# All values first in the second projections of a decoder layer, and the late half of a norm spread over two projections

## The chip, the cores and the metric

The kernel runs on one core of one Trainium2 chip. The metric is device time in microseconds (us) of one execution. The core has TensorE (PE, matrix products), VectorE (DVE) and ScalarE (ACT) for elementwise work, GpSimd (POOL), and SyncE (SP), from whose queue nearly all DMAs of this kernel are issued. PSUM banks hold the products of PE until ACT or DVE have read them.

## What is computed

One decoder layer in float32 on x (8 batches of 100 tokens, 1024 features) and a context of 8 x 722 tokens:

```python
x = layernorm(x + retention_attention(x))            # 8 heads, rope, gated, out projection
# cross attention: 16 query heads, 4 key/value heads of 128
q = rms_norm(x @ wq); k = rms_norm(x @ wk); v = x @ wv
k_ctx = rms_norm(ctx @ wk_ctx); v_ctx = ctx @ wv_ctx
q, k = rope(q), rope(k)
probs = softmax(q @ concat(k_ctx, k).T * scale + mask)
x = layernorm(x + (probs @ concat(v_ctx, v)) @ wo)
x = layernorm(x + (silu(x @ w_gate.T) * (x @ w_up.T)) @ w_down.T)
```

## The kernel before

Features lie on the 128 partitions, and the 800 tokens are worked in two halves of N = 400. Every float32 operand of a large product is split into a high part (an ACT cast) and a low part (a DVE subtraction; both are `split2`, line 68), and a product is three matmuls (`mm3`, lines 90, 93 and 94). `proj` multiplies a weight of 1024 x 128 with one half of the normed activations z: 8 steps of 3 matmuls into one PSUM bank. PSUM has three banks of tag "a", four of tag "s" and one of tag "v". `load_w` loads a weight into one of three staging tiles (`wst`) and splits it into one of four `w` tiles.

A scheduler of the framework orders the instructions of each engine ahead of time by its own simulation; on the chip every engine runs its instructions in that order. `pin` (`keep_in_program_order`) keeps the pinned instructions in the order of the program among themselves, and `issue_after(x)` puts what is issued within it behind x.

`out_proj` makes the output projection and the layer norm behind it, and is used twice: after the first attention (its z feeds the second projections) and after the cross attention (its z feeds the first products of the feed-forward part). For each half it computes eight blocks y[m]. The second half's norm is split. `norm_early`, in the middle of the eighth block, takes the mean of the first seven blocks (a product with `onem7`, L345), subtracts it (L347) and squares. What is left goes as a table of steps, `todo`, to the projection after it: the eighth block's share `delta` as a product (L302) before step QT = 4 of `proj`, the variance (L302) before step 7, and with it `late`: `norm_late` (L353, L356, L358), the inverse root (L127 to L135) and `scaled` (L322), which scales the eight blocks, splits them into z and writes them out.

The second projections (tile pool `l2`) are, for each of the four key/value heads kv, weights w2[kv, 0..3] for queries, w2[kv, 4] for keys and w2[kv, 5] for values. They go in groups of weights: for kv = 0 the four queries, then key and value; for the others two, two and two. Within a group come the first half of the tokens for all its weights, then the second. The very first projection, w2[0, 0] on the first half, is the one that carries `todo`. A query or key is squared on ACT (L701), summed over the partitions on POOL (L140), turned by rope (ACT copies L148 and L149; DVE products L150, L151 and sum L152; L150 is the last DVE reader of its bank), scaled by the inverse root (L127 to L135, L706), split into `d` and written out to `qd` or `kd`. A value is copied to `vt` by ACT (L160), transposed by PE in four pieces (L163), split into `vs` and written to `vd`.

The first batch's context is loaded and split by `load_context(0)`, called before the second group: eight loads of a `cs` tile (of the `wst` staging tiles), each with a split into `big`. The context's keys for kv = 0 and 1 are projected between the groups (`context_keys`), with weights read back from `wcd`.

In the feed-forward part the weights w3[i, part] for i = 0, 1 (gate and up) are multiplied with z of the first half and then of the second; the very first of these projections carries the second norm's `todo`.

Of the kernel before, what the change touches and what calls it, by code (L numbers as in the profile page):

```python
# [18 lines left out]
NB = 4  # L19
# [21 lines left out]
def decoder_layer(ctx, tc, xT, cT, w1, wo1, w2, wo2, wc, w3, wd, gw, qw, kw, trig, dec, mask, out):  # L41
# [68 lines left out]
            return True  # L110
        return False

    def proj(w, z, n=N, tag="a", todo=None):
        acc = bank(tag)[:, :n]
        for k in range(KT):
            pinned = between(todo, k)
            t = z[k // QT]
            mmw(acc, w, k, t[:, 0, k % QT, :n], t[:, 1, k % QT, :n], k == 0, k == KT - 1, pinned)
        return acc
# [32 lines left out]
        nc.vector.tensor_tensor(t1, t1, t2, op)  # L152
        return t1

    def tokens_first(pool, acc, copied=True):

        vt = acc
        if copied:
            vt = pool.tile([P, N], F32, tag="vt", name="vt", bufs=1)
            nc.scalar.copy(vt, acc)  # L160
        tr = bank("s")
        for b in range(NB):
            nc.tensor.transpose(tr[0:T, b * P:(b + 1) * P], vt[:, b * T:(b + 1) * T], ident)  # L163
        return tr[0:T]
# [70 lines left out]
    def out_proj(half, w, load_o, res, yp, ybufs, p, make_z, dst, z, steps={}):  # L235


        og = load_o(half)
        y = None
        s1 = p.tile([P, N], F32, tag="s1", name="s1", bufs=2)  # L240
        early = {}
        first = 4 if half == 0 else 1
        for ms in [range(first)] + [[m] for m in range(first, KT)]:
            accs = [bank(("aaasaaaa", "sssaaass")[half][m])[:, :N] for m in ms]
            todo = steps.get(ms[0])
            if half == 1 and KT - 1 in ms:
                todo = {QT: lambda: early.update(norm_early(y, s1, p))}
            for c in range(2):
                for m, acc in zip(ms, accs):
                    wt = load_w(w[m, c])  # L250
                    for k in range(KT):
                        kt = c * KT + k
                        pinned = between(todo, k) if c == 0 and m == ms[0] else False
                        rh, rl = og(kt)
                        a = acc if len(rh.shape) == 2 else bt(acc)
                        mmw(a, wt, k, rh, rl, kt == 0, kt == 2 * KT - 1, pinned)
            if y is None:
                y = yp.tile([P, KT, N], F32, tag="y", name="y", bufs=ybufs)
            for m, acc in zip(ms, accs):
                rs = yp.tile([P, N], F32, tag="rs", name="rs", bufs=2)  # L260
                nc.sync.dma_start(out=rs, in_=res[half, :, m])
                if early:
                    nc.vector.tensor_tensor(rs, rs, early["mean"], ALU.subtract)
                    with tc.high_priority():
                        nc.vector.tensor_tensor(y[:, m], acc, rs, ALU.add)
                else:
                    nc.vector.tensor_tensor(y[:, m], acc, rs, ALU.add)
                    add_up(s1, y, m)


        kept = {}

        def centre():
            kept["mean"] = bank("s")[:, :N]
            pin(nc.tensor.matmul(kept["mean"], onem, s1, start=True, stop=True))

        def less(ms):
            for m in ms:
                nc.vector.tensor_tensor(y[:, m], y[:, m], kept["mean"], ALU.subtract)
            kept["sq"] = squares(y, p, ms, kept.get("sq"))  # L280

        def whole():
            var = bank("v")[:, :N]
            pin(nc.tensor.matmul(var, onem, kept["sq"], start=True, stop=True))
            z.append(make_z(half))
            scaled(y, inv_root(p, var, eps_ln), lambda m: dst[half, :, m], z[half])

        def late():
            norm_late(y, early, p)
            z.append(make_z(half))  # L290
            scaled(y, inv_root(p, early["vs"], eps_ln), lambda m: dst[half, :, m], z[half])

        if half == 0:
            return {0: {QT: centre}, 1: {QT: lambda: less(range(QT))}, 2: {QT: lambda: less(range(QT, KT))},
                    4: {QT: whole}}, y
        sq = squares(y, p, [KT - 1])
        return {QT: lambda: summed(early["delta"], y[:, KT - 1], True, True),
                KT - 1: lambda: (summed(early["var"], early["sq"], True), summed(early["var"], sq, False, True), late())}, y

    def summed(acc, x, start=False, stop=False):  # L300

# [15 lines left out]
                s2 = s3  # L317
        return s2

    def scaled(y, r, dst, z=None):  # L320
        for m in range(KT):
            nc.vector.scalar_tensor_tensor(y[:, m], y[:, m], -0.5, r, ALU.mult, ALU.mult)  # L322
            if z is not None:
                split(z[m // QT][:, :, m % QT], y[:, m])
            nc.sync.dma_start(out=dst(m), in_=y[:, m])

    def norm_root(y, s1, p):
        n = y.shape[2]
# [289 lines left out]

    z1pool = sbuf("z1", 4)
    z1p = z1pool.__enter__()  # L620

    with sbuf("ln1", 1) as p:
        z1, todo = [], {}
        for half in range(2):
            todo, _ = out_proj(half, wo1, load_o1, xT, p, 2, p, lambda _: [
                z1p.tile([P, 2, QT, N], FR, tag="z", name="z") for _ in range(2)], zd, z1, todo)
        ws2 = [load_w(w2[0, 0])]
        acc2 = [proj(ws2[0], z1[0], todo=todo)]


    kapool = sbuf("ka", 2, "right")
    ka = kapool.__enter__()
    cz = []

    def load_context(b):

        cz.clear()
        for hf in range(2):
            n = SN[hf]
            z = [big([P, 2, QT, SH]) for _ in range(2)]  # L640
            for k in range(0, KT, 2):
                cs = wp.tile([P, KT * P], F32, tag="wst", name="cs", bufs=3)
                cs = cs[:, :2 * n].rearrange("p (k n) -> p k n", k=2)
                nc.sync.dma_start(out=cs, in_=cT[b, :, k:k + 2, hf * SH:hf * SH + n])
                split(z[k // QT][:, :, k % QT:k % QT + 2, :n], cs)
            cz.append(z)

    def context_keys(kv):

# [26 lines left out]


    early = []
    with sbuf("l2", 2) as p:
        for kv in range(NKV):  # L680
            for i0, i1 in ((0, 4), (4, 6)) if kv == 0 else ((0, 2), (2, 4), (4, 6)):
                if (kv, i0) == (0, 4):
                    load_context(0)
                ws = [ws2.pop() if ws2 else load_w(w2[kv, i]) for i in range(i0, i1)]
                if (kv, i0) in ((1, 2), (2, 2)):
                    step, kept = context_keys(kv - 1)
                    early.append(kept)
                if (kv, i0) in ((1, 2), (2, 0), (2, 2), (3, 0)):
                    step(i0 == 0)
                for half in range(2):  # L690
                    bs = slice(half * NB, (half + 1) * NB)
                    for i in range(i0, i1):
                        acc = acc2.pop() if acc2 else proj(ws[i - i0], z1[half])
                        if i == 5:
                            tr = tokens_first(p, acc).rearrange("p (b d) -> p b d", b=NB)
                            vs = p.tile([T, NB, 2, P], FR, tag="vs", name="vs", bufs=1)
                            split2(vs[:, :, 0], vs[:, :, 1], tr)
                            nc.sync.dma_start(out=f32(vd[kv, :, bs]), in_=f32(vs))
                            continue
                        sq = p.tile([P, N], F32, tag="sq", name="sq")  # L700
                        nc.scalar.activation(sq, acc, AF.Square)  # L701
                        ss = all_red(p, sq, "ss")
                        tb = tq if i < 4 else tk
                        t = rope(p, acc, tb[:, 0], tb[:, 1], swapped=bank("s")[:, :N])
                        r = inv_root(p, ss, eps_k, at=bank("s")[:, :N])
                        nc.vector.scalar_tensor_tensor(  # L706
                            t, t, -0.5 if i < 4 else -0.5 * math.sqrt(P), r, ALU.mult, ALU.mult)
                        d = p.tile([P, NB, 2, T], FR, tag="d", name="d", bufs=3)
                        split2(d[:, :, 0], d[:, :, 1], bt(t))
                        nc.sync.dma_start(out=f32(qd[kv, i, :, bs] if i < 4 else kd[kv, :, bs]), in_=f32(d))  # L710
    z1pool.__exit__(None, None, None)


# [157 lines left out]
    with sbuf("lnp2", 1) as p:  # L871
        z2, todo = [], {}
        for half in range(2):
            todo, y = out_proj(half, wo2, load_o2, zd, y2p, 1, p, make_z2, zd2, z2, todo)
        w0 = load_w(w3[0, 0])
        acc3 = [proj(w0, z2[0], tag=acc_tag(), todo=todo)]
        mixed2(y)
    zb["b11"], zb["b21"], zb["b22"] = z2[0][0], z2[0][1], z2[1][1]

# [5 lines left out]


    C = ("c11", "c12", "c21", "c22")
    ws = [[w0 if i == part == 0 else load_w(w3[i, part]) for part in range(2)] for i in range(2)]
    gs = {}
    for half in range(2):  # L890
        for i in range(2):
            ag, au = [acc3.pop() if acc3 else proj(w, z2[half], tag=acc_tag()) for w in ws[i]]
            t = temp()
            nc.scalar.activation(t, ag, AF.Silu)
            nc.vector.tensor_tensor(t, t, au, ALU.mult)
# [319 lines left out]
```

## Time and profile before

| | us |
|---|---|
| median of 4 runs | 2502.68 (2501.89 to 2506.67) |
| the profiled execution | 2503.55 |
| its span, first to last instruction | 2501.7 |
| PE busy | 2463.3 (98%) |
| DVE busy | 1950.2 (78%) |
| ACT busy | 1342.4 (54%) |
| POOL busy | 465.6 (19%) |

The profile is of one execution. Busy times are the union of an engine's instructions; a busy PE includes time at a lower granted clock. "Idle before" names the engine whose instruction ended an idle stretch. All positions in time below are microseconds from the start of the span. The first output projection ends at about 583, the second projections at about 837, the second output projection at about 1727.

### The profile page before, as it was taken

How to read it: one execution, taken by the hardware profiler on the slowest of the kernel's cores; microseconds unless marked ns; L12 is line 12 of the kernel's file. 1: busy time of each engine (PE TensorE's matmuls, PEld its weight loads, DVE VectorE, ACT ScalarE, POOL GpSimd, SP SyncE). 2: the span in 40 equal slices, each digit the busy share in tenths (PEclk: the TensorE clock that was granted, in tenths of full speed). 3: DMA queues.
4: the chain of work that ended last, by engine and by line, in shares of the span. 5: the costliest groups of instructions: out<-in, count | busy, mean ns of one | idle time of the engine just before them, and what ended most of it. 6: DMA issues, size and time to landing. Idle time of an engine off the chain costs nothing.

```text
span 2501.7 us, 37219 instructions
## 1 busy us (share of the span) xinstructions
PE 2463.3 (98%) x14068; PEld 2442.7 (98%) x14068; DVE 1950.2 (78%) x3101; ACT 1342.4 (54%) x2258; POOL 465.6 (19%) x234
## 2 busy tenths in 40 slices
PE   9999999997999999999999999999999999999997
PEld 9999999997999999999999999998999999999997
DVE  7778877567877688998999999857977777666756
ACT  6666676335777565665656656534544544432221
POOL 0111111002455343443433433100000000000000
PEclk9999999998999999999999999999999999999999
DMA  7333445774443654454455554565445444388731
GB/s 242 111 111 128 137 144 184 239 269 142 170 148 129 207 191 155 151 177 162 158 168 161 167 175 152 176 239 175 140 171 193 168 166 168 124 287 316 281 103 53
DMA packets 224451, 433.98 MB, mean 173 GB/s; under 512 B 47338, under 2 KB 168042, under 8 KB 211854
## 3 DMA queue, kind: packets, MB, share of 16 engines
q1 hardware_dynamic: 222542, 426.87, 50.2%
q0 software_dynamic: 1152, 4.19, 1.0%
q8 instruction: 111, 1.82, 0.3%
q14 instruction: 70, 0.57, 0.1%
q10 hardware_dynamic: 576, 0.52, 0.1%
HBM read 322.18 MB, written 109.35 MB: 172 GB/s over the span
## 4 chain that ended last, share of the span: by engine, by line
PE 95%; DVE 2%; DMA 1%; ACT 1%; POOL 0%; issue 0%; SPq 0%; DVEq 0%; ACTq 0%
PE a L94 20%; PE a L90 20%; PE a L93 20%; PE s L94 9%; PE s L93 9%; PE s L90 9%; PE v L94 2%; PE v L90 2%; PE v L93 2%; PE s L541 1%; PE s L744 1%; PE s L163 1%; DVE y L322 1%; PE v L533 0%; DMA w<-wcd 0%; POOL ss L140 0%
## 5 line engine op out<-in xcount | busy, mean ns | idle before, releaser
L90 PE MATMUL a<-big,w 128*128 128x400 f32 (+2 forms) x1808 | 609.6, 338 | 2.6 <-DMA w<-wcd 1.2
L93 PE MATMUL a<-big,w 128*128 128x400 f32 (+2 forms) x1808 | 609.2, 337 | 0.2 <-DVE big L68 0.2
L94 PE MATMUL a<-big,w 128*128 128x400 f32 (+2 forms) x1808 | 607.6, 337 | 0.4 <-DVE w L68 0.4
L68 ACT CAST w<-wst 128x1024 fp32r<-128x1024 f32 (+1 forms) x231 | 239.7, 1038 | 387.9 <-PE s L94 148.2
L68 DVE TENSOR_TENSOR w<-wst,w 128x1024 fp32r<-128x1024 f32 (+1 forms) x231 | 282.0, 1221 | 144.4 <-ACT w L68 142.9
L90 PEld LDWEIGHTS a<-big,w 128*128 128x128 f32 x1808 | 339.7, 188 | 5.1 <-DVE s L135 1.8
L93 PEld LDWEIGHTS a<-big,w 128*128 128x128 f32 x1808 | 340.2, 188 | 2.1 <-DVE big L68 0.8
L94 PEld LDWEIGHTS a<-big,w 128*128 128x128 f32 x1808 | 340.2, 188 | 1.2 <-DVE w L68 0.6
L90 PE MATMUL a<-z,w 128*128 128x400 f32 x680 | 236.0, 347 | 15.3 <-DVE t L150 15.3
L94 PE MATMUL a<-z,w 128*128 128x400 f32 x680 | 236.4, 348 | 0.0
L93 PE MATMUL a<-z,w 128*128 128x400 f32 x680 | 236.0, 347 | 0.0
L90 PE MATMUL s<-big,w 128*128 128x400 f32 x664 | 229.9, 347 | 0.1
L94 PE MATMUL s<-big,w 128*128 128x400 f32 x664 | 228.7, 346 | 0.4 <-DVE w L68 0.4
L93 PE MATMUL s<-big,w 128*128 128x400 f32 x664 | 228.9, 345 | 0.0
L140 POOL PARTITION_ALL_REDUCE ss<-sq x56 | 151.5, 2707 | 325.1 <-DMA zd<-y 166.1
L661 POOL PARTITION_ALL_REDUCE kss<-ksq x64 | 167.4, 2616 | 130.7 <-ACT ksq L660 130.1
L90 PEld LDWEIGHTS a<-z,w 128*128 128x128 f32 x680 | 128.8, 189 | 16.7 <-DVE t L150 13.8
L778 ACT ACTIVATE s<-s,rk 128x400 f32<-128x400 f32 x160 | 87.9, 592 | 93.6 <-DVE sm L798 67.2
L94 PEld LDWEIGHTS a<-z,w 128*128 128x128 f32 x680 | 129.4, 190 | 0.2
L93 PEld LDWEIGHTS a<-z,w 128*128 128x128 f32 x680 | 128.7, 189 | 0.5
L90 PEld LDWEIGHTS s<-big,w 128*128 128x128 f32 x664 | 124.6, 188 | 1.6 <-ACT w L68 0.4
L94 PEld LDWEIGHTS s<-big,w 128*128 128x128 f32 x664 | 125.1, 188 | 0.7 <-DVE w L68 0.7
(355 smaller groups left out, 5439.9 us busy)
## 6 DMA issues: line engine op xcount, KB each, us to landing
wst<-in_w SPq DMA_DIRECT2D x135, 512.0 KB
w<-wcd SPq DMA_DIRECT2D x64, 1024.0 KB
wst<-in_wo SPq DMA_DIRECT2D x64, 512.0 KB
hd<-h SPq DMA_DIRECT2D x12, 1400.0 KB
wst<-in_wd SPq DMA_DIRECT2D x64, 256.0 KB
big<-o1d SPq DMA_DIRECT2D x16, 800.0 KB
qd<-d SPq DMA_DIRECT2D x32, 400.0 KB
q<-qd SPq DMA_DIRECT2D x32, 400.0 KB
```

Source lines behind the costliest of these rows:

```text
L68: return nc.scalar.copy(hi, src), nc.vector.tensor_tensor(lo, src, f32(hi), ALU.subtract)
L90: i = nc.tensor.matmul(acc, lh, rh, start=start, stop=False, skip_group_check=chain)
L93: nc.tensor.matmul(acc, lh, rl, start=False, stop=False, skip_group_check=chain)
L94: nc.tensor.matmul(acc, ll, rh, start=False, stop=stop, skip_group_check=chain)
L140: nc.gpsimd.partition_all_reduce(y, x, P, op)
L163: nc.tensor.transpose(tr[0:T, b * P:(b + 1) * P], vt[:, b * T:(b + 1) * T], ident)
L322: nc.vector.scalar_tensor_tensor(y[:, m], y[:, m], -0.5, r, ALU.mult, ALU.mult)
L541: nc.tensor.matmul(bt(o)[:, b], vv[:, b * P:(b + 1) * P], pf[:, b], start=True, stop=True)
L661: nc.gpsimd.partition_all_reduce(ss[:, at], sq[:, at], P, RED.add)
L744: nc.tensor.transpose(tr[0:rows, (c - c0) * P:(c - c0 + 1) * P], vt[:, c * P:c * P + rows], ident)
L778: nc.scalar.activation(sc, sp, AF.Copy, scale=rk[:, c:c + 1])
```

## The change

- In the second projections a first group holds the value weights of all four kv. Their projections on the first half stand within the norm: `todo` is now a table per projection, delta before step 4 of the first, the variance before step 2 of the second, and `late` is called once the second value's products are issued. The first matmul of these two projections is pinned.
- `own_values` does what the loop did for a value, from a pool `v0` of its own, with two `vs` tiles. `late` gets the ACT copy of the second value, and each split of z stands behind it. The values of kv = 2 and 3 stand behind the last ACT cast of z.
- After the values of the second half come, for each kv, two queries, then two queries and the key.
- `load_context(0)` becomes `context_steps`: one of the eight load-and-split steps is issued ahead of each of the projections 4 to 11 (counted from the first value), from two staging tiles in pool `l2`, and each split stands behind the split pair of the projection before.
- In the feed-forward part the first two projections carry the norm's steps in the same way, and `late` follows both, without an instruction to stand behind.

```diff
-    def proj(w, z, n=N, tag="a", todo=None):
+    def proj(w, z, n=N, tag="a", todo=None, pinned=False):
         acc = bank(tag)[:, :n]
+        first = pinned
         for k in range(KT):
-            pinned = between(todo, k)
+            pinned = between(todo, k) or first and k == 0
...
-        return {QT: lambda: summed(early["delta"], y[:, KT - 1], True, True),
-                KT - 1: lambda: (summed(early["var"], early["sq"], True), summed(early["var"], sq, False, True), late())}, y
+        return {0: {QT: lambda: summed(early["delta"], y[:, KT - 1], True, True)},
+                1: {2: lambda: (summed(early["var"], early["sq"], True), summed(early["var"], sq, False, True))},
+                "late": late}, y
...
-            if z is not None:
+            if z is not None and behind is not None:
+                with tc.issue_after(behind.ins):
+                    cast = split(z[m // QT][:, :, m % QT], y[:, m])[0]
+            elif z is not None:
                 split(z[m // QT][:, :, m % QT], y[:, m])
...
+    def own_values(kv, half, acc):
+        got = []
+        tr = tokens_first(v0, acc, True, 1, got).rearrange("p (b d) -> p b d", b=NB)
+        vs = v0.tile([T, NB, 2, P], FR, tag="vs", name="vs")
+        last = split2(vs[:, :, 0], vs[:, :, 1], tr)
+        nc.sync.dma_start(out=f32(vd[kv, :, half * NB:(half + 1) * NB]), in_=f32(vs))
+        return got[0], last
...
-        ws2 = [load_w(w2[0, 0])]
-        acc2 = [proj(ws2[0], z1[0], todo=todo)]
+        ws2 = [load_w(w2[kv, 5]) for kv in range(NKV)]
+        for kv in range(NKV):
+            acc = proj(ws2[kv], z1[0], todo=todo.get(kv), pinned=kv < 2)
+            if kv < 2:
+                got, behind = own_values(kv, 0, acc)
+            else:
+                with tc.issue_after(cast.ins):
+                    got, behind = own_values(kv, 0, acc)
+            if kv == 1:
+                cast = todo["late"](got)
...
+                cs = pool.tile([P, KT * P if behind is None else 2 * SH], F32, tag="wst", name="cs", bufs=bufs)
...
+                    with tc.issue_after(behind[0].ins), tc.issue_after(behind[1].ins):
+                        split(to, cs)
...
-        for kv in range(NKV):
-            for i0, i1 in ((0, 4), (4, 6)) if kv == 0 else ((0, 2), (2, 4), (4, 6)):
-                if (kv, i0) == (0, 4):
-                    load_context(0)
+    groups = [[(kv, 5) for kv in range(NKV)]]
+    for kv in range(NKV):
+        groups += [[(kv, i) for i in range(2)], [(kv, i) for i in range(2, 5)]]
+    unit = NKV
...
+        ctx0 = context_steps(0, p, 2, behind)
+        for g, group in enumerate(groups):
+            ws = ws2 if g == 0 else [load_w(w2[kv, i]) for kv, i in group]
+            if g in (2, 5):
+                step, kept = context_keys(len(early))
+                early.append(kept)
+            if g in (2, 3, 5, 7):
+                step(g in (3, 7))
+            for half in range(g == 0, 2):
+                bs = slice(half * NB, (half + 1) * NB)
+                for (kv, i), w in zip(group, ws):
+                    if 4 <= unit < 12:
+                        next(ctx0)
+                    acc = proj(w, z1[half])
+                    unit += 1
+                    if i == 5:
+                        behind[:] = own_values(kv, half, acc)[1]
+                        continue
...
-        w0 = load_w(w3[0, 0])
-        acc3 = [proj(w0, z2[0], tag=acc_tag(), todo=todo)]
+        w0 = [load_w(w3[0, part]) for part in range(2)]
+        acc3 = [proj(w0[u], z2[0], tag=acc_tag(), todo=todo[u], pinned=True) for u in range(2)]
+        todo["late"]()
```

## The prediction

> **What bounds the kernel now.** I read the page's busy times first, then the list of waits for TensorE (PE), then the stretches around its waits, then the timelines of VectorE (DVE) and ScalarE (ACT) there.
>
> ```profile
> PE 2463.3 (98%) x14068; PEld 2442.7 (98%) x14068; DVE 1950.2 (78%) x3101; ACT 1342.4 (54%) x2258; POOL 465.6 (19%) x234
> ```
>
> PE is the bound: 2501.7 - 2463.3 = 38.4 us idle in all, some of it at the start and the end. No other engine can give anything except through PE's waits, so the next view is the waits (total, times, longest, in us).
>
> ```profile
> PE a L90 <- DVE t L150: 15.3, 2, 13.5
> PE s L93 <- DVE f L68: 3.0, 1, 3.0
> PE s L90 <- ACT f L68: 2.2, 1, 2.2
> PE a L90 <- DMA w<-wcd: 1.2, 2, 0.6
> ```
>
> The 15.3 us are two waits in the second projections, where a projection needs an accumulator bank that rope's first product (L150) still has to read. The 2.2 and 3.0 us lie at the start of the feed-forward part, where PE waits for the normed second half (tile f). These are the two places that the change touches. The same stretches by time show what a wait costs beside itself (columns: PE, PEld, DVE, ACT, POOL busy, then the granted clock, DMA share, GB/s):
>
> ```profile
> 596.00:609.50 13.50, 0.04 (x1) 0.00 (x0) 13.43 (x27) 8.04 (x16) 3.35 (x1) 0.65 0.71 252
> 609.50:613.30 3.80, 3.79 (x11) 3.75 (x12) 1.02 (x2) 1.78 (x4) 3.80 (x2) 0.50 0.00 0
> 638.00:640.00 2.00, 0.12 (x2) 0.07 (x1) 2.00 (x3) 1.01 (x3) 1.11 (x1) 1.00 0.38 148
> 640.00:644.50 4.50, 4.50 (x17) 4.47 (x18) 4.50 (x7) 3.05 (x6) 2.60 (x1) 0.62 0.36 117
> 780.00:828.00 48.00, 48.00 (x265) 48.00 (x264) 37.33 (x69) 34.97 (x70) 26.07 (x11) 1.00 0.47 164
> 1742.20:1748.30 6.10, 0.96 (x4) 0.48 (x3) 6.03 (x13) 4.34 (x9) 0.00 (x0) 0.89 0.57 179
> 1748.30:1753.00 4.70, 4.67 (x14) 4.63 (x15) 4.70 (x10) 3.19 (x6) 0.00 (x0) 0.50 0.94 332
> ```
>
> The row 780 to 828 is the undisturbed pace: 48.0 / 265 = 0.181 us a matmul, so a projection of 24 matmuls (a unit from here on) takes 4.35 us. After each wait the clock stands at 0.50 for some microseconds: lost are 3.8 x 0.50 = 1.9, 4.5 x 0.38 = 1.7 and 4.7 x 0.50 = 2.35 us (with the 0.95 of the next 7 us, 2.7). So the waits and their clock cost 13.47 + 1.9 + 1.88 + 1.7 = 19.0 us at the first place and 2.18 + 2.99 + 2.7 = 7.9 us at the second. 26.9 us is the ceiling of what this change can bring.
>
> Why the long wait exists is in DVE's and PE's timelines:
>
> ```profile
> 601.12 3.97 DVE L322 SCALAR_TENSOR_TENSOR y<-y,r 128x400 f32<-128x400 f32 x8
> 605.01 3.96 DVE L68 TENSOR_TENSOR z<-y,z 128x400 fp32r<-128x400 f32 x8
> 608.90 0.56 DVE L150 TENSOR_TENSOR t<-a,tq 128x400 f32<-128x400 f32 x1
> ...
> 609.51 0.70 PE L90 MATMUL a<-z,w 128*128 128x400 f32 x1 [13.47 <-DVE t L150]
> ```
>
> From 583.3 (the end of the last output projection) PE does three units on the first half's z, fills the three banks of tag a, and stops at 596.0: the rope of the first query stands behind the whole norm on DVE.
>
> **The change part by part.** Same matmuls, transposes, casts and bytes; only places and order move. I take the new order with the durations of before.
>
> *Values first, within the norm (first place).* A value needs no rope: ACT copies the bank (0.49 us, L160), PE turns it (4 transposes in 0.35 us), ACT casts (0.59) and DVE subtracts (0.69). Banks are thus freed by ACT, which was busy 8.0 of the 13.5 us. The 14 z matmuls that stood before the mean (573.55 to 576.1) can't go there any more, as unit 0 is pinned; PE reaches the mean at 573.7. Its operand s1 was ready at 572.8, so no wait, and the mean, with DVE's chain behind it, comes 2.5 us earlier. Last output projection: ends 583.3 - 2.5 = 580.8. Unit 0's first 12 matmuls: 582.9. Delta (0.7): 583.6. 12 + 6 matmuls: 586.9, where the variance stands. Its operand: before, DVE went from the first L347 (576.96) to the last sum of squares (590.5) in 13.6 us, of which 2.5 were three context splits and 1.25 an idle time for one; without these 9.9 us, from 574.5 to 584.4, or 585.6 with one more weight split. So it is there 1.3 us early; I book 0.7 us for a small wait, bounds 0 and 3.6 (a 1.9 us wait with the 1.7 us of clock that the wait at 638 cost).
>
> Variance 1.3 us: 588.2. Then, as before, subtraction, Ln, Exp, Square and two DVE steps: 595.3 to 601.1 = 5.8 us before, of which 1.3 went to a context split in front; so scaling starts at about 592.7 and z's eight parts are done by about 601.4 (8 us, and one value's 0.69). PE meanwhile: 18 matmuls of unit 1 to 591.5, units 2 and 3 to 600.2, transposes 0.7: it asks for the first part of z at 600.9, when seven of eight are there, and takes one each 0.54 us. No wait, with little to spare at the last part. The cover here is the four value units, 17.4 us; were it gone, the 13.5 us would be back.
>
> The added waits: z's casts stand behind the copy of value 1 (at about 592.0, before the first scaled y: nothing). Values 2 and 3 stand behind the last z cast (about 601); behind them on PE wait transposes, and the bank of value 2 is needed by the unit that starts at 605: 3 us to spare. The second vs tile takes away a wait that ACT had for vd's write (2.9 us in 780 to 828), off PE's path: nothing.
>
> *Weights and SP's queue.* Four value weights use the four w tiles; two become free when the last output projection passes its two weights (about 576 and 581), and are needed at 591 and 596: covered by 10 us. The eight context loads, which stood on SP from 573.9 to 594.5 ahead of three weights, go behind them: that helps the weights. In their new place each load waits on SP for one of two tiles that its split two units earlier frees (8.7 us against 3.5 to 4.3 us waited for a load at 583 and 591), with writes of qd and weight loads behind it.
>
> *Context's steps in units 4 to 11.* Eight splits, 0.8 us on ACT, 0.83 pitch on DVE. A query unit costs DVE 3.64 us (32.8 us of 37.3 in 780 to 828 for nine) and half a weight split (0.57): 4.2 of 4.35. With a context split 5.0; units 4 to 7 are values (about 2.1 with a split), units 8 to 11 run behind by 4 x 0.7 = 2.8 us. A bank must be free two units (8.7 us) after its unit ends, so this is hidden; the key products of context (4.1 us of PE for 0.6 of DVE) give it back.
>
> *Forty query and key units in a row.* DVE: 40 x 3.64 + 20 x 1.14 + 4 x 0.5 = 170 us; ACT: 40 x 3.55 + 20 x 1.05 + 4 x 0.9 = 167; PE: 40 x 4.35 + 4 x 4.1 = 190. Eleven such units ran at 780 to 828 without a wait. Nothing, therefore; the waits on wcd (1.2 us) stay.
>
> *The feed-forward place.* The variance stood at PE's 1738.1 though its operand was ready at 1734.1. Now two units are pinned behind the mean, so the 24 matmuls done at 1715.3 can't cover the mean's wait: s1 was ready only at 1717.6, because residual loads came late:
>
> ```profile
> 1716.42 0.57 DVE L267 TENSOR_TENSOR y<-s,rs 128x400 f32<-128x400 f32 x1 [0.87 <-DMA rs<-zd]
> 1717.03 0.57 DVE L306 TENSOR_TENSOR s<-s,y 128x400 f32<-128x400 f32 x1
> ```
>
> PE waits 1717.6 - 1715.3 = 2.3 us there. Clock lost by that: between 0 and 1.9; I take 1.7, the row of the wait nearest in length (1.88 us). The chain then runs: mean 1717.7, projection to 1724.9, delta 1727.8, variance 1731.1 (operand 13 us after the mean, 1731) to 1732.5; first part of f 8.6 us later as before, 1741; PE has 18 + 48 matmuls to 1744.5. Both old waits go. Net 7.9 - 2.3 - 1.7 = 3.9 us.
>
> On that clock: the trace has 0.50 after a wait of only 1.88 us. The Trainium skill, "TensorE: Matmul & The Clock Gate", HAM oscillation, asks only that idle gaps stay below about 3.4 us; by it a 2.3 us wait would lose no clock, and the sum would be 1.7 us better. The same page (Architectural detail) calls ACT and DVE strict FIFO, which speaks against pinning more on ACT; the row that bears on it is the Ln at 597.23, behind a context cast that waited 1.29 us for its load.
>
> **The sum.** 19.0 - 0.7 + 3.9 = 22.2 us. The profiled execution took 2503.55 us (span 2501.7 and 1.85 around it): 2481.35. It lies 0.87 above the median of 2502.68, so 2480.5.
>
> **Rivals.**
> *A, the norm still ends last.* If the scheduler's order puts weight splits or values' splits between the norm's steps on DVE (each 0.5 to 1.2 us), z comes 4 to 8 us later than 601 and PE waits that long, plus 1.9 of clock; or the variance waits. For: DVE was busy 13.43 of 13.50 us there. Against: the context splits, 6.6 us, are gone. Time 2480.5 + 6 to 10, or with both places hit up to 2497.
>
> *B, no change in sum.* The order PE, ACT and DVE run in is fixed ahead; an order that fits badly, with waits of about 2 us and 1.7 of clock each, five or six of them, eats it: 2498 to 2507.
>
> *C, slower: the query stretch becomes DVE's and ACT's.* From 614.0 to 644.1 six query units, each with a weight split, advanced at 5.0 us a unit (L150 to L150), the 1.88 us wait within. If forty units went at that pace: 40 x 0.65 = 26 us, against 22.2 less the 3.6 us of that wait already counted: 2503 - 18.6 + 26 = 2510. It decides where a unit's DVE or ACT work with its bubbles passes 4.35 us. Against: half a weight split a unit, and the eleven units without a wait.
>
> **How the numbers follow.** Forecast (2473 to 2488) 0.60, A 0.20, B 0.09, C 0.11. Within 0.2% (about 5 us, what a measurement of this kernel can tell) is B: faster 0.80, same 0.09, slower 0.11. The low end is the ceiling with the 0.87 us and the wcd waits: 2502.7 - 26.9 - 2 = 2474; the high end takes in A: 2497. That leaves out about 2 in 10.
>
> **What would show it.** Right: PE's waits on L150 and on f gone, clock 1.00 through the second projections, values' matmuls at 581 to 600, the first use of the second half's z at about 601 with no idle before it, a wait of about 2 us on s1's product before the feed-forward part. Wrong: a PE wait on z or on a variance product (A), on L150 in the query units (C), or on context's loads (B).

## The result, and the profile after

The changed kernel takes 2507.3 us (median of 42 runs, 2504.78 to 2510.7) against 2503.35 us before (60 runs): ratio 1.0015, 95% interval 1.0011 to 1.0020, so 0.15% slower, where 0.9% faster was forecast. The profiled execution took 2507.49 us, its span 2505.6.

The first view after is again PE's waits (total, times, longest, us):

```profile
PE a L90 <- DMA w<-wcd: 7.6, 1, 7.6
PE a L90 <- ACT z L68: 3.5, 1, 3.5
PE a L93 <- DVE z L68: 2.9, 1, 2.9
PE a L90 <- ACT s L131: 2.6, 1, 2.6
PE s L355 <- DVE s L311: 2.5, 1, 2.5
...
PE s L93 <- DVE f L68: 1.1, 1, 1.1
PE s L90 <- DVE s L821: 1.0, 1, 1.0
```

The two waits on rope that held 15.3 us are gone. In their place stand new ones: on z of the second half (3.5 and 2.9), on a weight read back from `wcd` (7.6), on something that the list calls ACT (2.6, at 737), and the foreseen one on s1 (2.5). The waits by time, with the stretch behind each (columns as in the prediction):

```profile
602.60:609.50 6.90, 0.58 (x2) 0.19 (x1) 6.83 (x15) 4.95 (x11) 0.00 (x0) 0.87 0.45 162
609.50:614.30 4.80, 4.77 (x16) 4.60 (x17) 4.06 (x8) 1.42 (x4) 0.00 (x0) 0.50 0.82 264
649.40:657.10 7.70, 0.09 (x1) 0.03 (x1) 7.70 (x13) 5.83 (x12) 2.60 (x1) 0.67 0.87 296
657.10:662.30 5.20, 5.20 (x17) 5.20 (x18) 4.84 (x9) 1.45 (x3) 0.00 (x0) 0.50 0.40 159
737.40:740.20 2.80, 0.15 (x1) 0.03 (x1) 2.35 (x5) 2.54 (x5) 2.02 (x1) 1.00 0.92 381
740.20:744.20 4.00, 4.00 (x15) 4.00 (x16) 4.00 (x8) 2.79 (x6) 0.59 (x1) 0.57 0.54 94
1721.00:1723.60 2.60, 0.13 (x1) 0.03 (x1) 1.50 (x3) 0.00 (x0) 0.00 (x0) 1.00 0.86 275
1723.60:1727.40 3.80, 3.79 (x10) 3.14 (x11) 2.27 (x5) 1.02 (x2) 0.00 (x0) 0.55 0.32 106
```

With the clock (time at half speed times a half), the waits on z cost 6.35 + 2.4 us, the one on `wcd` 7.6 + 2.6, the one at 737 2.65 + 1.7.

Where the 3.9 us of the two spans arise, by marks in PE's timeline: the first norm's mean product (576.09 before with 14 later matmuls, 2.5 us, already done; 574.16 after), the first score product (845.32; 849.59), the second norm's mean product (1719.70 with 24 matmuls, 4.4 us, already done; 1723.61) and the end. Up to the first mark +0.6, second projections +3.7, cross attention up to the second mean +4.0 (2.5 of it the wait for s1, which belongs to the feed-forward change, and 1.0 the wait on L821), the rest -4.4. So the feed-forward part gained 1.9 us, and the second projections, where 18.3 us were to be gained, lost 3.7.

Why z is late stands in DVE's timeline of the changed kernel:

```profile
585.36 0.57 DVE L321 TENSOR_TENSOR s<-s,sq 128x400 f32<-128x400 f32 x1 [0.34 <-ACT sq L316]
588.44 0.69 DVE L68 TENSOR_TENSOR vs<-s,vs 100x512 fp32r<-100x512 f32 x1 [2.50 <-ACT vs L68]
598.81 0.69 DVE L68 TENSOR_TENSOR vs<-s,vs 100x512 fp32r<-100x512 f32 x1 [9.68 <-ACT vs L68]
599.42 2.00 DVE L363 TENSOR_TENSOR y<-y,s 128x400 f32<-128x400 f32 x4
...
605.01 3.97 DVE L328 SCALAR_TENSOR_TENSOR y<-y,r 128x400 f32<-128x400 f32 x8
608.91 3.96 DVE L68 TENSOR_TENSOR z<-y,z 128x400 fp32r<-128x400 f32 x8
```

The sums of squares end at 585.9, a little later than the 585.6 of the prediction, and PE makes the variance at 588.7 to 590.2. Then DVE does nothing for 9.7 us: the next instruction of its queue is the subtraction of the second value, which waits for ACT's cast, which waits for that value's four transposes. These stand on PE 23 matmuls into the third unit (597.55), although ACT's copy was made at 594.1:

```profile
597.55 0.60 PE L166 MATMUL s<-ident,vt 128*100 128x128 f32 x4
```

The norm's L363, whose operand had been there since 584.4, is behind.

Why the weight is late stands in SP's timeline:

```profile
649.10 0.34 SPq L74 DMA_DIRECT2D wst<-in_w  x1
649.53 0.38 SPq L84 DMA_DIRECT2D w<-wcd  x1
...
733.21 0.36 SPq L84 DMA_DIRECT2D w<-wcd  x1
```

PE ended the second query of the first query group at 649.5; that freed the fourth `w` tile, the load went out at 649.53, and PE's next instruction was the product that reads it, at 657.1. The load of 733.21 and the product at 740.2 are the same again, though the list names ACT.

### The profile page after: what moved, and what is told of

It reads as the page before. It is cut to its first block, busy times and chain, and to the rows that moved or that the text cites. A ratio compares the mean times of both kernels' runs of the same rounds, so it can differ in the third digit from the quotient of the medians.

```text
span 2505.6 us, 37218 instructions
## 1 busy us (share of the span) xinstructions
PE 2466.1 (98%) x14068; PEld 2444.6 (98%) x14068; DVE 1949.6 (78%) x3101; ACT 1341.6 (54%) x2258; POOL 464.6 (19%) x234
## 4 chain that ended last, share of the span: by engine, by line
PE 94%; DMA 3%; DVE 2%; ACT 1%; issue 0%; SPq 0%; DVEq 0%; ACTq 0%
PE a L94 20%; PE a L93 20%; PE a L90 20%; PE s L94 9%; PE s L93 9%; PE s L90 9%; PE v L94 2%; PE v L90 2%; PE v L93 2%; PE s L551 1%; PE s L791 1%; PE s L166 1%; DVE y L328 1%; PE v L543 0%; DMA wst<-in_wo 0%
## 5 line engine op out<-in xcount | busy, mean ns | idle before, releaser
L90 PEld LDWEIGHTS a<-big,w 128*128 128x128 f32 x1808 | 341.0, 189 | 14.7 <-DVE s L136 7.9
```

Of the source, the lines that this page charges most:

```text
L90: i = nc.tensor.matmul(acc, lh, rh, start=start, stop=False, skip_group_check=chain)
```

## The experiments

All ratios are to the kernel before, run on the same chip. Differences to the changed kernel go by its median of 2507.3 us, taken in other runs; the medians of the kernel before beside all of them lie within 0.8 us of each other. The first four change the changed kernel in one place each. Only the main lines of each edit are shown, with `...` where lines are left out.

**The norm ahead of the second value** (`then` is called behind the ACT copy in `tokens_first`, and `late` is given there):

```diff
-                got, behind = own_values(kv, 0, acc)
+                casts = []
+                norm = (lambda copy: casts.append(todo["late"](copy))) if kv == 1 else None
+                got, behind = own_values(kv, 0, acc, norm)
...
             if kv == 1:
-                cast = todo["late"](got)
+                cast = casts[0]
```

> Edit: the norm's late steps are issued right behind the second value's ACT copy, ahead of that value's transposes and split; all else as changed. Theory (DVE runs its queue in order, and the second value's subtraction, which waited 9.7 us for its transposes and cast, stood ahead of the norm's L363): DVE starts the norm's subtractions at about 590 in place of 599.4, the waits of PE on z (3.5 and 2.9 us) go, with the 1.9 us of clock behind them: 2507.3 - 8.3 = 2499. Rival (the pinned order of z's casts behind the ACT copy of the second value holds the norm): the copy comes at 594 in both, so at most 1 us changes: 2506. Rival (the query stretch is bound by ACT and DVE): the start moves, the end does not: 2507.

Measured: 2500.57 us, ratio 0.9985 (0.9976 to 0.9994). Both waits on z are gone, and DVE goes on without a gap:

```profile
587.60 0.69 DVE L68 TENSOR_TENSOR vs<-s,vs 100x512 fp32r<-100x512 f32 x1 [2.50 <-ACT vs L68]
588.21 2.00 DVE L365 TENSOR_TENSOR y<-y,s 128x400 f32<-128x400 f32 x4
590.13 0.56 DVE L370 TENSOR_TENSOR vs<-v,vs 128x400 f32<-128x400 f32 x1
...
593.82 3.97 DVE L330 SCALAR_TENSOR_TENSOR y<-y,r 128x400 f32<-128x400 f32 x8
```

From the delta product to the first score product PE needs 257.6 us in place of 266.1: 8.5 less, against 8.3 expected; in the medians 6.7. The first theory holds, and the pinned casts did not hold the norm.

**The key weight one group earlier:**

```diff
-            if g in (2, 5):
-                step, kept = context_keys(len(early))
-                early.append(kept)
             if g in (2, 3, 5, 7):
                 step(g in (3, 7))
+            if g in (1, 4):
+                step, kept = context_keys(len(early))
+                early.append(kept)
```

> Edit: the context's key weight is read back from wcd one group earlier (with groups 1 and 4 in place of 2 and 5), its product stays where it was. Theory (the weight gets the fourth w tile only when the last query of the group before has ended, at 649.5, and its load takes 7.3 us while PE stands at its product; the second such product at 737.6 the same): both waits (7.6 and 2.65 us) go, with the clock at 0.50 behind each (about 2.6 and 1.9 us): 2507.3 - 14.7 = 2492.5. Rival (the wait at 737.6 is ACT's, as the list names it, and the query stretch is bound by ACT and DVE): only the first wait goes, and part of it comes back in the stretch: 2498 to 2507.

Measured: 2497.85 us, ratio 0.9975 (0.9966 to 0.9985), 9.5 us below the changed kernel where 14.7 were expected. Both waits are gone, that at 737 too, so it was the load's and not ACT's; the list of the next run, where nothing changed here, names `wcd` for it (2.9 us). The same stretch is 253.2 us, 12.9 less. What is missing from 14.7 is two short waits at the place where context's last splits meet the first queries, and they are DVE's:

```profile
PE a L90 <- DVE kall L705: 1.3, 1, 1.3
...
PE a L90 <- DVE t L151: 0.6, 1, 0.6
```

Another part of the gain was lost at the start of the cross attention, where the wait on L821 grew from 1.0 to 2.2 us, and s1 was waited for 3.4 us in place of 2.5. The profiled execution was the slowest of the ten (2501.07 us), so these two need not be as large in the others.

**The feed-forward part as before** (`out_proj` hands back the old table there, one weight, nothing pinned):

```diff
...
-        acc3 = [proj(w0[u], z2[0], tag=acc_tag(), todo=todo[u], pinned=True) for u in range(2)]
-        todo["late"]()
+        acc3 = [proj(w0[0], z2[0], tag=acc_tag(), todo=todo)]
...
```

> Edit: the feed-forward part's first projections carry the norm as before the change (delta and variance in one projection, nothing pinned ahead); the second projections as changed. Theory (the feed-forward part of the change gained 1.8 us, by the shift of the two traces from 5.7 us ahead of it to 3.9 us at the end): 2507.3 + 1.8 = 2509. Rival (the feed-forward change lost time by its new wait for s1, 2.5 us): 2505 or less.

Measured: 2509.37 us, ratio 1.0021 (1.0012 to 1.0030), 2.1 us above the changed kernel. That agrees with the 1.9 us of the marks, though the intervals of the two ratios overlap. The old waits on f are back (2.4 and 2.2 us).

**The feed-forward part unpinned:**

```diff
-todo=todo[u], pinned=True) for u in range(2)]
+todo=todo[u]) for u in range(2)]
```

> Edit: the first matmuls of the two feed-forward projections are not pinned, so that they may be put ahead of the mean; all else as changed. Theory (the new wait of 2.5 us for s1, with the clock at 0.50 behind it until 1727.4, is the price of that pin): 2507.3 - 2.5 - 1.6 = 2503, less if the norm's chain then starts later and f is waited for again (2.2 and 3.0 us before). Rival (the pin costs nothing, since the norm's chain decides): 2507.

Measured: 2508.05 us, ratio 1.0015 (1.0006 to 1.0024): no gain. Six matmuls were put ahead of the mean, and the wait for s1 shrank to 0.9 us, but the wait for f grew from 1.1 to 2.2 us, by what six matmuls of 0.18 us take, and this time the clock fell behind that one:

```profile
1723.50:1724.40 0.90, 0.03 (x2) 0.02 (x1) 0.79 (x2) 0.00 (x0) 0.00 (x0) 1.00 0.81 173
1724.40:1728.00 3.60, 3.60 (x18) 3.31 (x19) 2.64 (x6) 1.40 (x3) 0.00 (x0) 1.00 0.44 155
1750.90:1753.10 2.20, 0.05 (x1) 0.00 (x0) 2.20 (x6) 2.18 (x5) 0.00 (x0) 1.00 0.93 277
1753.10:1758.00 4.90, 4.88 (x18) 4.86 (x19) 4.90 (x11) 3.18 (x6) 0.00 (x0) 0.65 0.91 320
```

The expectation missed its middle and met its proviso: covering the wait by matmuls that are then lacking later moves it.

**Both mends together:**

> Edit: both mends together, the norm's late steps ahead of the second value's transposes and the key weight of the context one group earlier. Theory (the two losses are independent waits of PE): 2507.3 - 6.7 - 9.5 = 2491, the two measured gains added, and 2488 if the waits and their clock go in full (8.3 and about 10.5). Rival (what one mend gains comes back in the query stretch, which ACT and DVE bound): 2495 or more.

Measured: 2482.91 us, ratio 0.9922 (0.9908 to 0.9936): 24.4 us below the changed kernel, more than the two gains added. The stretch is 242.2 us, 23.8 less; r1's and r2's own gains there make 21.3. The two short waits on DVE that r2 had are absent here, and the wait at the start of the cross attention, 2.1 us in r1 and 2.2 in r2, is 1.1. For the queries the stretches of this kernel answer rival C:

```profile
610.00:650.00 40.00, 40.00 (x230) 39.78 (x229) 28.52 (x44) 27.59 (x50) 15.88 (x6) 1.00 0.68 219
650.00:800.00 150.00, 150.00 (x832) 150.00 (x831) 137.05 (x239) 123.32 (x242) 90.18 (x38) 1.00 0.44 153
```

PE is busy for 150 of 150 us at full clock, with DVE at 137 (91%) and ACT at 123 (82%).

**A third tile for the residual blocks, with both mends** (`rs` with bufs=3 in `out_proj` and `mixed2`):

> Edit: both mends, and three tiles in place of two for the residual blocks (rs) that the output projections add. Theory (s1 is late in the second output projection because the load for the seventh block waits for the tile of the fifth): PE's wait for s1 (2.5 us) goes with its clock (about 1.6): 4 us below the kernel with both mends alone. Rival (s1 is late because DVE is busy with the first half's norm): the wait stays, 0 to 1 us.

Measured: 2478.25 us, ratio 0.9900 (0.9887 to 0.9914), 4.7 us below the kernel with both mends. The wait for s1 is gone from the list, so it came from the load's wait for its tile. This is the fastest of the versions, 1.0% below the kernel before and 1.2% below the changed one.

**Both mends without the order on ACT:**

```diff
-                norm = (lambda copy: casts.append(todo["late"](copy))) if kv == 1 else None
+                norm = (lambda copy: todo["late"]()) if kv == 1 else None
...
-                with tc.issue_after(cast.ins):
-                    got, behind = own_values(kv, 0, acc)
+                got, behind = own_values(kv, 0, acc)
```

> Edit: both mends, and none of the pinned order on ACT: z's casts are not put behind the second value's copy, nor the values of kv = 2 and 3 behind the last of z's casts. Theory (the order on ACT costs and gains nothing, since the copy was done before the first scaled block): within 1 us of the kernel with both mends. Rival (the order keeps values 2 and 3 out of the norm's way on DVE): the norm ends 1 to 3 us later and PE waits on z again: 2 to 5 us more. Rival (the order costs): 1 to 2 us less.

Measured: 2487.01 us, ratio 0.9938 (0.9926 to 0.9951), 4.1 us above the kernel with the order, though the two intervals overlap. The size is that of the first rival, the place is not: PE waits nowhere on z, but 1.3 us on the key product's bank, 0.6 on L151 and 2.5 at the start of the cross attention. So the order seems to be worth some 4 us here; by which step it keeps DVE ahead at 640 to 660 is not shown.

**Context's steps two by two** (with both mends and the third tile; `4 <= unit < 8` and `next(ctx0)` twice):

> Edit: both mends and the third rs tile, and context's eight steps two by two in the four value projections of the second half (4 to 7) in place of one by one in 4 to 11. Theory (DVE falls behind in projections 8 to 11, where a context split is added to a query: the waits of 0.6 us on L151 and 1.3 us on the key product's bank): both go, about 2 us below the same kernel with steps one by one. Rival (two staging tiles can't be loaded and split in 4.4 us): ACT waits for loads, the key product's operand comes late, 2 to 6 us more.

Measured: 2480.53 us, ratio 0.9908 (0.9895 to 0.9922), 2.3 us above the kernel with single steps; the intervals overlap. The wait on the key product's bank is 1.8 us here and absent there. The theory's gain did not come: the two waits that it was to remove were already absent with single steps.

## Why the prediction was wrong, step by step

- **The diagnosis held.** With PE's waits on rope and most of those on f taken away without new long ones in their place, the kernel is 25 us faster than before (the third tile for residual blocks included), near the ceiling of 26.9. That its 2478.25 us lie near the forecast of 2480.5 is no merit of the forecast, which was for the change alone.
- **The step that failed first** is "Then, as before, ... scaling starts at about 592.7 and z's eight parts are done by about 601.4". Its durations were about right: with both mends scaling starts at 592.99, 20.2 us after the mean product where 19.0 were foretold, and the last part of z ends at 601.45. But it took DVE's queue as if the norm's steps could go when their operands were there, and put the second value's split at its own 0.69 us. In the changed kernel that subtraction stands ahead of the norm's steps and held DVE for 9.7 us, so that the wait on z, which the sum had at nothing, cost 8.5 us by r1. Rival A foretold this wait, for splits between the norm's steps, and its 6 to 10 us hold the 8.5, though it priced the splits by the 0.5 to 1.2 us each takes and not by what they wait for. The strict FIFO that the prediction cited from the Trainium skill ("TensorE: Matmul & The Clock Gate", Architectural detail) agrees with this gap. The row that the prediction gave for it bears on it only indirectly: the Ln at 597.23 waited 1.46 us for DVE's L358, which stood behind the split of that context cast.
- **The second is a term left out.** "the waits on wcd (1.2 us) stay": the four `w` tiles were followed for the value weights alone. With a group of three weights and the context's key weight behind two query weights, the fourth tile comes free only as PE reaches the product. Two waits, 10.3 us and some 4 of clock; r2 gives 12.9 us of PE's stretch. No rival had this loss.
- **Rival B's time came without its mechanism.** 2507.3 us lies 0.3 above its 2498 to 2507, but the gain was eaten by A's wait and by the two on `wcd`, not by five or six waits of 2 us. That is luck.
- **Rival C is refuted:** with both mends PE is busy from 610 to 824 without a gap, at full clock, through all query and key units. The prediction's argument against C was weaker than it says: of the eleven units at 780 to 828 only nine were queries or keys, the others a value and a key product of the context.
- **The feed-forward step** forecast 3.9 us and gave 1.9 (marks) to 2.1 (r3). The wait for s1 was 2.47 us against 2.3, and its clock 3.8 x 0.45 = 1.7 as taken; in r1 the same wait of 2.53 us lost none, so that term was not sure. What failed is "variance 1731.1": it came at 1743.7, 20.1 us after the mean and not 13.4. The order on PE puts 24 matmuls of the third unit ahead of it (4.4 us), and its operand, booked 13 us after the mean, came after 16.1, the lost clock within (the kernel before has 14.4: 1719.70 to 1734.14). So 1.1 us of the wait on f stayed; the rest of the 2 us that are missing has no cause shown.
- **The cover of the second vs tile, of SP's move and of context's steps** was as told, but for the waits of 1.3 and 0.6 us in r2, which the prediction had at nothing.

## What to carry to other kernels

Before work is moved into an engine's idle time, write down that engine's new queue in order, with what each entry waits for: an entry costs the whole wait of its operand to all that stands behind it, here 9.7 us for a subtraction of 0.69. Count the tiles of a rotating buffer through the whole new order, with the loads that share them: a load that takes the last tile is issued when its reader is already due. And when a wait is covered by work, ask whether that work was the cover of a later one.

## What the runs showed of the chip that was not expected

A short wait of PE sometimes lowers its clock and sometimes does not. After 1.88 us (before) it fell to 0.50, after 2.47 us (the changed kernel's wait for s1) to 0.55 over 3.8 us, after 2.17 us (unpinned feed-forward) to 0.65 over 4.9 us. After 2.19 us in r2 it stayed at 1.00:

```profile
844.80:847.00 2.20, 0.05 (x1) 0.00 (x0) 0.39 (x2) 0.00 (x0) 0.00 (x0) 1.00 0.99 339
847.00:849.00 2.00, 1.96 (x11) 1.96 (x12) 1.96 (x5) 0.23 (x1) 0.00 (x0) 1.00 0.44 180
```

The place alone does not decide it. In r1 the same product waits for s1 for 2.53 us, a little longer than in the changed kernel, and the clock stays at 1.00:

```profile
1713.00:1715.56 2.56, 0.03 (x1) 0.03 (x1) 1.85 (x3) 0.00 (x0) 0.00 (x0) 1.00 0.76 224
1715.56:1720.00 4.44, 4.44 (x22) 4.15 (x23) 3.49 (x8) 2.07 (x3) 0.00 (x0) 1.00 0.34 123
```

The Trainium skill, "TensorE: Matmul & The Clock Gate", Part 1, describes a free-running window of about 3.4 us, and says that the moment at which the clock rises at a kernel's start depends on where in the window the first matmul lands. If the same held for a wait, its phase would decide, and these rows of about 2 us could differ as they do; that was not tested. The page's idle window of about 3.4 us before the clock falls does not fit the rows, in which it fell after 1.88 to 2.47 us.
